# Tokens for the attention product: turned by VectorE in 32 by 32 blocks from a quartered load, instead of by TensorE

## The chip, the core and the metric

The kernel runs on one core of one Trainium2 chip. The metric is the device time of one launch in microseconds (us). Three runs of the kernel before gave 1968.97, 1972.87 and 1973.47 us; the median is 1972.87 us. All times below are from these runs or from one further execution that the hardware profiler recorded.

## What is computed

The reference takes x (4 batches of 1024 rows by 1024 features, float32) and a context (4 batches of 1024 by 512). Cut to what matters:

```python
query = ctx @ Wq.T + bq;  key = ctx @ Wk.T + bk            # 1024 x 128 for each batch
attention = softmax(query @ key.T, axis=-1)                # 1024 x 1024
x = x + einsum('bln,bmn->blm', layernorm(x), attention)    # rows l, features n and m
x = x + moe_ffn(layernorm(x))                              # shared and 8 routed experts
```

The rows of x are the tokens. Their features n are the index that the product with the attention sums over, so attention's second axis and the features of x must lie in the same order, whichever order that is. The normalisation is applied after the product: the raw x goes into the product, and the result is scaled by the row's reciprocal deviation and added to x minus its scaled mean.

## The kernel before, in words

The 4096 tokens are 32 tiles of 128 rows, numbered g. The first stage (some 640 us of the profile) makes attention and the product with it; the rest is the shared and the routed feed-forward network.

**The loop.** The first stage runs over pairs of token tiles, g = 0, 2, ..., 30; four pairs make a batch b. `product` (L399) multiplies the pair's two token tiles with the batch's attention by a scheme of seven block products instead of eight (`seven`, L197). Step k is eight matmuls of 128x512, into the PSUM banks pa, pc, pa, pb, pa, pc, pa. After step k VectorE adds the finished bank to x (L410, called "add k" below), and `between(k)` puts in the other work of the pair: the next batch's energies, softmax and turning of attention (`energies`, `softmax`, `turned`, only in the first three batches), the second normalisation and its turning of the previous pair (`second_norm` L426, `turn` L434), routing (`route` L460), lists, scatter. Since one bank serves several steps, step 4 needs add 2, step 6 needs add 4, and step 0 of the next pair needs add 6.

**Tokens.** TensorE sums over partitions, so a token tile must stand with features on partitions. `load(g)` (L374) reads the 128x1024 tile, rows on partitions. `tokens(g)` (L379) calls `transposed` (L250): eight TensorE transposes (L256) of 128x128 into two PSUM banks named pt_x, and two ScalarE copies (L260) of 128x512 into xT. `tokens(g + 1)` stands at the head of the pair (L611), `tokens(g + 2)` in `between(5)` (L684). `row_sums(g)` (L391, lines 176 to 179) then makes on GpSimd the four sums of the pair's blocks that the steps 1, 2, 4 and 5 use; it stands at the head of the pair (L613).

**After the add.** `stored(g)` (L421) follows add 5 and add 6: it writes the tile to x2d and takes its statistics on VectorE (L266 to 271); GpSimd makes rs and nb of them (L273, L275), and ScalarE the normalised tile xt (L430). `turn(g - 2)`, at the head of the next pair in the first three batches (L622), turns this xt on TensorE (pt_t). At the end of a batch VectorE also makes two sums of the next attention (L357, L362), and GpSimd two more (L367, L368).

**What sets the order.** On TensorE, GpSimd, VectorE and ScalarE each engine works in the order in which the code is written. The order of SP's queue, which issues all plain loads and stores, is set by a planner from its own costs; SP takes its entries one after the other and waits at each until what it needs is there. In the prologue (L540 to L587) SP loads weights, the first context blocks ct, constants, x, and gw_sb (L563), whose tile VectorE must have cleared first (L562).

The three lines that matter most:

```python
tokens(g + 1)              # L611, head of the pair
first_norm(g + 1)
a_units = row_sums(g)      # L613
```

Of the kernel before, what the change touches and what calls it, by code (L numbers as in the profile page):

```python
# [28 lines left out]
F32 = mybir.dt.float32  # L32
# [8 lines left out]
P = 128  # L41
B, S, D = 4, 1024, 1024
C = 512
T = B * S
NT = T // P
# [32 lines left out]
def xattn_moe_kernel(ctx: ExitStack, tc: tile.TileContext, x, ctxT, wqT, wkT, bqk, gwT, ebias,  # L78
                     w13, w2, w2t, sw13, sw2, sw2t, consts, out):
    nc = tc.nc  # L80
# [142 lines left out]


    HALF, KH, M = KC // 2, NF // 2, NF * P
    LT = S // P
    with ExitStack() as a:
        p1 = pool(attention, "p1")
# [7 lines left out]
        p4 = pool(two_sums, "p4", 1, "right")  # L236
# [13 lines left out]
        def transposed(dsts, src, n, second=None):  # L250

            for h, dst in enumerate(dsts):
                pt = ps_t.tile([P, HALF, P], F32, tag="pt", name=f"pt_{n}_{h}")
                for j in range(HALF):
                    c = h * HALF + j
                    nc.tensor.transpose(pt[:, j, :], src[:, c * P : (c + 1) * P], ident)  # L256
                if h and second:
                    nc.vector.tensor_copy(dst, pt)
                else:
                    nc.scalar.copy(dst, pt)  # L260
# [36 lines left out]
        def half_queries(b):  # L297
            for h in range(2):
                pq = ps_e.tile([P, 2, 2, 256], F32, tag="pe", name=f"pq_{b}_{h}")
                for j in range(2):  # L300
                    k = 2 * h + j
                    if (k, 0) not in contexts:
                        for i in range(2):
                            load_context(b, k, i)
                    ct = [contexts.pop((k, i)) for i in range(2)]
                    for i, w in enumerate((wq_sb, wk_sb)):
                        for c in range(CC):
                            nc.tensor.matmul(pq[:, i, j, :], w[c // CH][:, c % CH, :],  # L308
                                             ct[c // CH][:, c % CH, :],
                                             start=c == 0, stop=c == CC - 1)  # L310
                cols = slice(h * 512, (h + 1) * 512)
                for i, to in enumerate((qs, ks)):
                    nc.vector.tensor_scalar_add(
                        to[b][:, cols], pq[:, i].rearrange("p j n -> p (j n)"), bqk_sb[:, i : i + 1])
                yield

        def energies(b, m):
# [51 lines left out]
            t_sums[b] += four,  # L369


        xin, xTs, x1s, xts, norms = {}, {}, {}, {}, {}

        def load(g):  # L374
            x1 = p3.tile([P, D], F32, tag="x1", name=f"x1_{g}", bufs=4)
            nc.sync.dma_start(x1, x[g * P : (g + 1) * P, :])
            xin[g] = x1

        def tokens(g):  # L379
            xTs[g] = [p3.tile([P, HALF, P], F32, tag=f"x{g % 2}{h}", name=f"xT_{g}_{h}")  # L380
                      for h in range(2)]
            transposed(xTs[g], xin[g], f"x{g}")

        def first_norm(g):

# [164 lines left out]
            load_context(0, 1, i)  # L550
        nc.sync.dma_start(con, consts)
        load(0)
        with tc.manual_schedule(engines=vector_scalar):
            ps_e = psum("ps_e", 3)
            for dst, k in ((trib, "tri"), (onesb, "ones")):
                nc.vector.tensor_copy(dst, const(k))
            halves = queries(0)
            tokens(0)
            norms[0] = statistics(xin[0], "1_0")
            first_norm(0)  # L560
            gw_sb = wp.tile([P, KC, 32], F32, name="gw_sb")
# [7 lines left out]
            nc.sync.dma_start(eb_sb, ebias)  # L569
            next(halves)  # L570
            load(1)
            norms[1] = statistics(xin[1], "1_1")
            for m in range(LT + 2):
                if m < LT:
# [7 lines left out]
                if 0 < m <= LT:  # L582
                    scaled(0, m - 1, on_scalar=False)
            next(halves)
            first_sums(0)
            second_sum(0)
            ps_a.close()  # L587
# [3 lines left out]
            for p in range(NT // 2):  # L591
                g = 2 * p
                b, i = divmod(g, LT)
                ahead = b + 1 < B
                if g == NT - LT:

                    attention.close()
                    cps.append(pool(shared, "c0"))
                    sw13_sb = cps[0].tile([P, KC, W13], F32, name="sw13_sb")
                new = ahead and i == 0 and b > 0  # L600
                nms = {}

                def looked(m):
                    if ahead:
                        nms[m] = energies(b + 1, m)

                def softened(m):
                    if ahead:
                        softmax(b + 1, m, nms[m])

                tokens(g + 1)  # L611
                first_norm(g + 1)
                a_units = row_sums(g)  # L613
                if i == 0:
                    last_sums(b)
                if new:
                    halves = queries(b + 1)
                else:
                    looked(i)
                if p:  # L620
                    if ahead:
                        turn(g - 2)  # L622
                    second_norm(g - 1)
                if not new:
                    softened(i)

                def between(k):
                    if k == 0:
                        if not ahead:
                            turn(g - 2)  # L630
                        if new:
                            next(halves)
                        if p > 1:
                            pc_, ss, ohs = listing[g - 4]
                            listing[g - 4] = lists_of(g - 4, pc_, ohs), ss
                        if g + 2 < NT:
                            load(g + 2)
                            load(g + 3)
                        if g == NT - LT:
                            nc.sync.dma_start(sw13_sb, sw13)  # L640
                    elif k == 1:
                        if new:
                            looked(i)
                            softened(i)
                        if p:
                            turn(g - 1)
                        if ahead:
                            scaled(b + 1, i, on_scalar=True)
                        if p > 1:
                            tois, ss = listing.pop(g - 4)  # L650
                            listing[g - 4] = tois, [weighted(g - 4, j, ss) for j in range(G)]
                        if p in (1, 3, 5, 7, 10, 13):
                            convert((1, 3, 5, 7, 10, 13).index(p))
                    elif k == 2:
                        if not ahead:
                            pair[g] = gate_parts(g - 2)
                        looked(i + 1)
                        softened(i + 1)
                        if g + 2 < NT:
                            norms[g + 2] = statistics(xin[g + 2], f"1_{g + 2}")  # L660
                        if g + 2 == NT:
                            two_sums.close()
                            cps.append(pool(shared, "c3"))
                            block(0)
                    elif k == 3:
                        if p:
                            gs = gate_parts(g - 2) if ahead else pair.pop(g)
                            lg = ps_s.tile([P, G, E], F32, tag="lg", name=f"lg_{g}")
                        if ahead:
                            turned(b + 1, i)  # L670
                            scaled(b + 1, i + 1, on_scalar=True)
                        if p:
                            gate(lg, gs)
                            routing[g - 2] = route(g - 2, lg)
                        if p > 1:
                            scatter(g - 4, *listing.pop(g - 4))
                        if g + 2 < NT:
                            norms[g + 3] = statistics(xin[g + 3], f"1_{g + 3}")
                    elif k == 4:
                        if ahead:  # L680
                            turned(b + 1, i + 1)
                    elif k == 5:
                        if g + 2 < NT:
                            tokens(g + 2)  # L684
                        if p:
                            mask, ss, ohs = routing.pop(g - 2)
                            pc_ = ps_s.tile([P, 2, G, E], F32, tag="lg", name=f"pc_{g}")
                            counts(pc_, mask)
                            listing[g - 2] = pc_, ss, ohs
                        if ahead and i + 2 == LT:  # L690
                            first_sums(b + 1)
                        second_norm(g)
                        if g + 2 < NT:
                            first_norm(g + 2)
                    elif k == 6:
                        if ahead and i + 2 == LT:
                            second_sum(b + 1)

                product(g, b, a_units, between)


            last_in.close()
# [576 lines left out]
```

## Time and profile before

| what | value |
|---|---|
| median of three runs | 1972.87 us |
| the profiled execution | 1973.84 us |
| its span, first to last instruction | 1972.0 us |
| mean granted TensorE clock | 0.996 |
| busy: TensorE, VectorE, ScalarE, GpSimd | 98%, 41%, 26%, 33% |
| the first stage, 0 to 650 us: TensorE busy | 635.4 us |
| the first stage: VectorE, ScalarE, GpSimd busy | 384.7, 274.2, 251.3 us |
| DMA traffic | 365.48 MB |

The profile's page lists engines, the span in 40 slices, the chain of work that ended last, and groups of instructions with count, busy time and mean duration. A timeline lists instructions of one engine in order: start in us, duration in us, engine, source line, operation, output<-input, shape, count, and in square brackets how long the engine was idle just before and what released it. TensorE's matmuls are pipelined: the duration of one reaches past the start of the next, so the time that a group costs is the distance from its start to the next group's start.

### The profile page before, as it was taken

The numbers are of one execution on the slowest core, as the hardware profiler recorded it, in microseconds if no ns is written. First come the engines' busy times: TensorE is split into PE (matmuls) and PEld (weight loads), VectorE is DVE, ScalarE is ACT, GpSimd is POOL, SyncE is SP. The second block draws the span as 40 slices with busy tenths as digits, with TensorE's granted clock in tenths as the row PEclk, the third lists the DMA queues.
The fourth block names the chain that finished last, engine by engine and source line by source line (L and its number), as shares of the span: only waits on it lengthen the run. The fifth ranks groups of instructions, "written<-read, shape, count | busy, mean of one in ns | idle before, by whom it ended". The sixth has DMA issues, their size and how long they took to land.

```text
span 1972.0 us, 23197 instructions
## 1 busy us (share of the span) xinstructions
PE 1940.1 (98%) x8480; PEld 1155.5 (59%) x8595; DVE 810.4 (41%) x1981; ACT 512.9 (26%) x884; POOL 653.0 (33%) x598
## 2 busy tenths in 40 slices
PE   8999999999999999999999999999999999999997
PEld 5655655655444447676676758584845555446564
DVE  5556566565875325423132323222233333223343
ACT  3344354355334101010111101010102233223242
POOL 0423533543642140313231222313014454425454
PEclk9999999999999999999999999999999999999999
DMA  3276485437685225397777868596464598649995
GB/s 124 65 194 169 167 220 158 154 129 206 246 228 203 98 75 141 94 238 205 202 187 191 206 179 224 153 173 193 121 265 107 114 311 275 140 131 326 342 357 98
DMA packets 225040, 365.48 MB, mean 185 GB/s; under 512 B 114080, under 2 KB 169888, under 8 KB 214048
## 3 DMA queue, kind: packets, MB, share of 16 engines
q0 software_dynamic: 43024, 172.78, 32.8%
q1 hardware_dynamic: 181904, 191.21, 32.0%
q8 instruction: 69, 1.13, 0.2%
q14 instruction: 43, 0.35, 0.1%
HBM read 289.19 MB, written 174.59 MB: 235 GB/s over the span
## 4 chain that ended last, share of the span: by engine, by line
PE 89%; DMA 5%; SPq 2%; DVE 2%; issue 1%; ACT 0%; POOL 0%; POOLq 0%; DVEq 0%; ACTq 0%
PE pa L129 19%; PE bank L129 15%; PE pc L129 10%; PE bank L1151 8%; PE qa L129 6%; PE pb L129 5%; DMA xh<-xgt 4%; PE pu L129 4%; PE pq L308 3%; PE pe L320 3%; PE qc L129 3%; PE pt_c L129 2%; PE pt_a L256 2%; SPq L1004 2%; PE qb L129 1%; PE pt_t L256 1%
## 5 line engine op out<-in xcount | busy, mean ns | idle before, releaser
L129 PE MATMUL bank<-xTb,w 128*128 128x0 bf16 x2024 | 311.6, 315 | 2.1 <-ACT sg_b L145 1.3
L129 PEld LDWEIGHTS <-w 128*128 128x128 bf16 x2024 | 190.5, 98 | 111.5 <-DVE hTb L1135 1.3
L749 POOL DMA_INDIRECT xgt<-xrows,li x92 | 88.8, 965 | 444.2 <-DMA xh<-xgt 211.6
L1184 POOL DMA_INDIRECT out_dram<-yt,toks x92 | 147.7, 1605 | 139.5 <-DVE yt L1180 80.8
L1151 PE MATMUL bank<-w,hTb 128*128 128x0 bf16 x920 | 164.5, 326 | 0.1
L273 POOL TENSOR_TENSOR rs<-ve,con 128x1 f32<-128x1 f32 x64 | 47.8, 747 | 313.7 <-DVE ve L271 313.7
L146 DVE TENSOR_TENSOR hTb<-sg_b,bank 128x512 bf16<-128x512 f32 x115 | 78.8, 688 | 161.5 <-PE bank L129 157.2
L129 PE MATMUL pa<-xs,sw_sb 128*128 128x256 f32 x560 | 132.3, 379 | 0.0
L1151 PEld LDWEIGHTS <-hTb 128*128 128x128 bf16 x920 | 72.4, 98 | 87.4 <-issue 11.7
L129 PE MATMUL pa<-aT,xT 128*128 128x512 f32 x256 | 116.8, 599 | 2.2 <-DVE x L410 2.0
L129 PEld LDWEIGHTS pa<-xs,sw_sb 128*128 128x128 f32 x560 | 106.4, 190 | 14.5
L145 ACT ACTIVATE sg_b<-bank 128x512 f32<-128x512 f32 x115 | 68.5, 597 | 165.8 <-PE bank L129 150.2
L1180 DVE COPY yt<-bank 128x512 f32<-128x512 f32 x92 | 61.3, 689 | 121.9 <-PE bank L1151 112.5
L1182 ACT COPY yt<-bank 128x512 f32<-128x512 f32 x92 | 53.3, 587 | 144.1 <-PE bank L1151 131.7
L749 POOL DMA_INDIRECT w<-w13b,wi x23 | 23.0, 999 | 201.4 <-PE bank L129 153.6
L534 POOL DMA_INDIRECT xrows<-rr,toi x64 | 64.9, 1015 | 60.9 <-issue 45.3
L410 DVE SCALAR_TENSOR_TENSOR x<-pa,rs,x 128x512 f32<-128x512 f32 x64 | 47.9, 748 | 88.8 <-PE pa L129 82.9
L166 ACT ACTIVATE st_c<-pt_c 64x256 f32<-64x256 f32 x7 | 2.6, 378 | 311.0 <-PE pt_c L129 311.0
L266 DVE BATCH_NORM_STATS2 st<-x 128x6 f32<-128x512 f32 x128 | 81.8, 681 | 0.6
L1032 DVE TENSOR_TENSOR x2c<-x2c,qa 128x512 f32<-128x512 f32 x64 | 43.8, 685 | 92.4 <-PE qa L129 92.4
L129 PE MATMUL pu<-xb,sw_sb 128*128 128x512 f32 x176 | 76.3, 593 | 0.9 <-PE pt_t L256 0.9
L941 DVE TENSOR_TENSOR one<-one,pb 128x256 f32<-128x256 f32 x35 | 14.7, 421 | 149.4 <-PE pb L129 140.1
(262 smaller groups left out, 3346.5 us busy)
## 6 DMA issues: line engine op xcount, KB each, us to landing
xturned<-xh SPq DMA_DIRECT2D x46, 512.0 KB
xTb<-xturned SPq DMA_DIRECT2D x23, 1024.0 KB
w13b<-in_w_dram POOLq DMA_DIRECT2D x8, 2816.0 KB
x<-in_x_dram SPq DMA_DIRECT2D x32, 512.0 KB
x2d<-x SPq DMA_DIRECT2D x32, 512.0 KB
xtd<-xtT SPq DMA_DIRECT2D x16, 1024.0 KB
xb<-xtd SPq DMA_DIRECT2D x8, 2048.0 KB
x2c<-x2d SPq DMA_DIRECT2D x16, 1024.0 KB
```

Source lines behind the costliest of these rows:

```text
L129: nc.tensor.matmul(part(pp), w(c), part(xT(c)), start=start and c == 0, stop=c == blocks - 1, skip_group_check=not start)
L145: nc.scalar.activation(sg, pa, AF.Silu)
L146: nc.vector.tensor_tensor(hT[:, f, :], sg, pb, ALU.mult)
L256: nc.tensor.transpose(pt[:, j, :], src[:, c * P : (c + 1) * P], ident)
L266: nc.vector.bn_stats(st[:, h, :], src[:, h * 512 : (h + 1) * 512])
L308: nc.tensor.matmul(pq[:, i, j, :], w[c // CH][:, c % CH, :], ct[c // CH][:, c % CH, :], start=c == 0, stop=c == CC - 1)
L320: nc.tensor.matmul(pe[:, h, :], qs[b][:, m * P : (m + 1) * P], ks[b][:, h * 512 : (h + 1) * 512], start=True, stop=True)
L534: nc.gpsimd.indirect_dma_start(out=places[2 * (g + i) + k], out_offset=bass.IndirectOffsetOnAxis(ap=tois[k][:, i : i + 1], axis=0), in_=rr ...
L749: nc.gpsimd.indirect_dma_start(out=dst, out_offset=None, in_=src, in_offset=bass.IndirectOffsetOnAxis(ap=idx, axis=0), **bound)
L1151: nc.tensor.matmul(part(py), hT[:, f, toks], part(w[:, f, cols]), start=False, stop=f == NF - 1, skip_group_check=q < 2)
L1180: nc.vector.tensor_copy(yt[:, q, h * 512 : (h + 1) * 512], py)
L1184: adds.append([nc.gpsimd.indirect_dma_start(out=outs[q], out_offset=bass.IndirectOffsetOnAxis(ap=toks[:, q : q + 1], axis=0), in_=yt[:, q, ...
```

## The change

A second copy of each token tile is loaded, cut in four: partition 32j + a of the new tile xq holds, for i = 0 to 3, features 256j to 256j + 255 of row 32i + a. That takes four DMAs of 128 KB for each token tile. VectorE then turns each half of xq with one instruction of 128x512 that transposes every 32 by 32 block in place. The result stands in xT in another order of features: partition 32j + f of block c holds feature 256j + 32c + f. So that attention has the same order, the keys are written in that order when the bias is added to them. TensorE's transposes of x and ScalarE's copies are gone.

The places change too. Tokens for the next pair are now turned in `between(4)` and `between(5)`, the next pair's `row_sums` is called in `between(6)` instead of at its head, and the first two tiles are turned after the prologue instead of in it.

```diff
-                for i, to in enumerate((qs, ks)):
-                    nc.vector.tensor_scalar_add(
-                        to[b][:, cols], pq[:, i].rearrange("p j n -> p (j n)"), bqk_sb[:, i : i + 1])
+                nc.vector.tensor_scalar_add(
+                    qs[b][:, cols], pq[:, 0].rearrange("p j n -> p (j n)"), bqk_sb[:, :1])
+                nc.vector.tensor_scalar_add(
+                    ks[b].rearrange("p (c j f) -> p j c f", j=4, f=SQ)[:, 2 * h : 2 * (h + 1)],
+                    pq[:, 1].rearrange("p j (c f) -> p j c f", f=SQ), bqk_sb[:, 1:])
...
+        def load_quarters(g):
+
+            xqs[g] = xq = p4.tile([P, 4, D // 4], F32, tag="xq", name=f"xq_{g}", bufs=2)
+            src = x[g * P : (g + 1) * P, :].rearrange("(i a) (j f) -> j a i f", a=SQ, j=4)
+            for j in range(4):
+                nc.sync.dma_start(xq[j * SQ : (j + 1) * SQ], src[j])
+
         def tokens(g):
             xTs[g] = [p3.tile([P, HALF, P], F32, tag=f"x{g % 2}{h}", name=f"xT_{g}_{h}")
                       for h in range(2)]
-            transposed(xTs[g], xin[g], f"x{g}")
+            src = xqs.pop(g).rearrange("p i (h c f) -> p h i c f", h=2, f=SQ)
+            for h, dst in enumerate(xTs[g]):
+                nc.vector.transpose(dst.rearrange("p c (i a) -> p i c a", a=SQ), src[:, h])
...
         load(0)
+        load_quarters(0)
...
-            tokens(0)
...
             load(1)
+            load_quarters(1)
...
             next(halves)
+            tokens(0)
+            tokens(1)
+            units = [row_sums(0)]
             first_sums(0)
...
-                tokens(g + 1)
                 first_norm(g + 1)
-                a_units = row_sums(g)
...
                         if g + 2 < NT:
-                            load(g + 2)
-                            load(g + 3)
+                            for h in (g + 2, g + 3):
+                                load(h)
+                                load_quarters(h)
...
                     elif k == 4:
                         if ahead:
                             turned(b + 1, i + 1)
+                        if g + 2 < NT:
+                            tokens(g + 2)
                     elif k == 5:
                         if g + 2 < NT:
-                            tokens(g + 2)
+                            tokens(g + 3)
...
                     elif k == 6:
+                        if g + 2 < NT:
+                            units[0] = row_sums(g + 2)
...
-                product(g, b, a_units, between)
+                product(g, b, units[0], between)
```

More of the change, by code (lines that the diff above doesn't have):

```diff
@@ L225, in xattn_moe_kernel @@
     HALF, KH, M = KC // 2, NF // 2, NF * P
+    SQ = P // 4
     LT = S // P
@@ L369, in last_sums @@
             t_sums[b] += four,
-        xin, xTs, x1s, xts, norms = {}, {}, {}, {}, {}
+        xin, xqs, xTs, x1s, xts, norms = {}, {}, {}, {}, {}, {}
         def load(g):
```

## The prediction

> **What bounds the kernel now.** I read the engines' busy times, the chain that ended last, busy times by 50 us, and then the timelines of TensorE (PE), VectorE (DVE), ScalarE (ACT) and GpSimd (POOL) around the places that the change touches.
>
> ```profile
> PE 1940.1 (98%) x8480; PEld 1155.5 (59%) x8595; DVE 810.4 (41%) x1981; ACT 512.9 (26%) x884; POOL 653.0 (33%) x598
> ...
> PE 89%; DMA 5%; SPq 2%; DVE 2%; issue 1%; ACT 0%; POOL 0%; POOLq 0%; DVEq 0%; ACTq 0%
> ```
>
> TensorE is the chain. Between 100 and 500 us of the windows it is never idle, so work taken from it there is time won, as long as nothing else becomes late. The end of one pair (g = 4) and the start of the next, on TensorE:
>
> ```profile
> 159.54 1.04 PE L256 MATMUL pt_x<-con,x 128*128 128x128 f32 x8
> ...
> 160.47 3.68 PE L129 MATMUL pa<-t,xT 128*128 128x512 f32 x8
> 163.98 1.04 PE L256 MATMUL pt_x<-con,x 128*128 128x128 f32 x8
> 164.86 1.88 PE L320 MATMUL pe<-kT,qT 128*128 128x512 f32 x4
> 166.58 1.04 PE L256 MATMUL pt_t<-con,xt 128*128 128x128 f32 x8
> 167.45 3.60 PE L129 MATMUL pa<-aT,xT 128*128 128x512 f32 x8
> 170.88 3.60 PE L129 MATMUL pc<-t,s 128*128 128x512 f32 x8
> ```
>
> Eight transposes take 0.87 us (163.98 to 164.86), not eight times their 273 ns, since they are pipelined. What the other engines do then:
>
> ```profile
> 158.72 0.74 DVE L410 SCALAR_TENSOR_TENSOR x<-pa,rs,x 128x512 f32<-128x512 f32 x1
> 159.74 0.75 DVE L410 SCALAR_TENSOR_TENSOR x<-pc,rs,x 128x512 f32<-128x512 f32 x1 [0.28 <-PE pc L129]
> 160.41 1.28 DVE L266 BATCH_NORM_STATS2 st<-x 128x6 f32<-128x512 f32 x2
> ...
> 164.19 0.75 DVE L410 SCALAR_TENSOR_TENSOR x<-pa,rs,x 128x512 f32<-128x512 f32 x1 [1.94 <-PE pa L129]
> ```
>
> ```profile
> 167.61 1.27 POOL L176 TENSOR_TENSOR s<-xT,xT 128x512 f32<-128x512 f32 x1
> ```
>
> ```profile
> 163.12 1.24 ACT L430 ACTIVATE xt<-x,nb,rs 128x1024 f32<-128x1024 f32 x1 [1.87 <-POOL nb L275]
> ```
>
> VectorE is busy without a gap from routing (153.3) to add 4 (158.72); behind that it has 0.28 us to spare before add 5 and 1.94 before add 6. That is all the room for new work. The last batch, with no next attention to prepare, has less cover on TensorE. And the prologue:
>
> ```profile
> 15.70 1.04 PE L256 MATMUL pt_x<-con,x 128*128 128x128 f32 x8
> 16.58 1.89 PE L308 MATMUL pq<-ct,wq_sb 128*128 128x256 f32 x8
> ```
>
> ```profile
> 10.53 5.74 SPq L294 DMA_DIRECT2D ct<-in_ctxT_dram  x4
> 16.32 0.94 SPq L376 DMA_DIRECT2D x<-in_x_dram  x2
> 19.30 0.69 SPq L563 DMA_DIRECT2D gw_sb<-in_gwT_dram  x1
> ```
>
> Four context blocks are issued from 10.53 on, in time for TensorE at 16.58. The load of gw_sb comes later, at 19.30, when VectorE has cleared its tile (19.00 to 19.27).
>
> **The parts.** Listed in order, the built kernel has 256 transposes fewer on TensorE, 64 copies fewer on ScalarE, 64 transposes more on VectorE (two after add 4, two after the statistics that follow add 5), the same order on GpSimd, and 128 more DMAs on SP.
>
> *One VectorE transpose.* The trace has none. Bounds from rows of float32 on VectorE: below, half of a 1024-wide scaling from SBUF (L340, 754 ns), 0.38 us; above, one reduction of 1024 elements (L323, 1224 ns), 1.22 us, as if each element took two turns. Nearest is L266, which reads 512 elements from SBUF: 681 ns, two in a row 1.28 us. I take 0.70 us, and 1.3 us for the two of a tile.
> The trace has no transpose to weigh a rule against. The Trainium skill, "VectorE: DVE Perf Modes", The three transpose paths, gives VectorE 311 ns for 128x128 bf16 and TensorE 390 ns; its Rules for kernel authors send a 128x128 transpose to TensorE all the same. [...]
>
> *TensorE's saving.* 32 tiles x 0.87 = 27.8 us if all of it counted. Two tiles fall in the prologue, the rest at the 15 seams between pairs: 1.74 us each.
>
> *Eight usual seams (not at a batch's end, first three batches).* The first two transposes start at 159.4, so add 5 moves from 159.74 to 160.7, the statistics, nb and xt by the same 0.95: xt ends at 165.3 instead of 164.36. TensorE, 1.74 earlier, wants xt for pt_t at 164.84: it waits 0.5. Then add 6 follows the other two transposes, at 164.5 to 165.2, in time for step 0 at 166.2; GpSimd's first row sum ends 169.2, step 1 wants it at 169.65. Won: 1.74 - 0.5 = 1.2 us, eight times, **-9.6**.
>
> *The first seam (g = 0 to 2)* has no routing on VectorE: xt ends by 95.3, TensorE wants it at 95.9: **-1.7**. *The seams 6 to 8 and 14 to 16* have 6.9 us of context products on TensorE at their head as cover; but GpSimd's sums of attention start some 2 us later and hold up small VectorE work: L525 took 4.37 us instead of 0.75 beside L367 at 514.57. I charge 0.5 each: 2 x (1.74 - 0.5), **-2.5**.
>
> *Last batch.* At 22 to 24 step 0 waits for add 6, which follows two transposes and L357: 503.21 becomes 505.4. Nothing covers it: **+2.2**, and the row sums behind it shift alike. At 24 to 26 VectorE is behind: add 4 ends 533.3 and the transposes go straight onto add 5, the statistics and add 6, while TensorE idles: +1.15. At 26 to 28 and 28 to 30 add 6 ends 0.2 later than the old transposes let step 0 start. Together **+3.75**.
>
> *Prologue.* In the new order of SP the load of gw_sb stands ahead of the four context blocks. It still waits for VectorE's clear at 19.27, which itself follows the first key and the statistics of tile 0. So the blocks are issued from about 20.5, not 10.53. The first load of the trace took 2.5 us from the end of its issue (1.62) to its first matmul (4.15); I add the same: TensorE goes on at 23.4 instead of 16.58, **+6.8** (bounds: 5.7 if the block lands in 1.4 us, 8.5 if the 1024 small packets of gw_sb hold it up). TensorE is then idle for 7.7 us. The only idle time so long is the start, and after it eight matmuls took 3.62 us at 8.58 and 1.89 us at 13.98; if it comes back so, 2 to 4 us are lost, if not, none: I take **+2**.
> The Trainium skill, "TensorE: Matmul & The Clock Gate", Why this matters for your kernels, says that a gap of over 3 us between bursts halves the clock again; the rows of the start agree with a slow beginning, and no row here shows it after a gap; by that rule and the start's 8 us the loss is 4.
> After the loop, four transposes (2.6 us) stand before L357, which step 1 needs: GpSimd and VectorE then share out L357, L362 and the row sums as at 64 to 71 us, and steps 1 and 2 come 0.55 late each, **+1.1**. The two old transposes of the prologue win nothing: the first lies in the new gap, the second in a wait for kT (0.72 us at 64.58).
>
> *Without cost:* the 128 DMAs (16.8 MB). SP issues one in 0.33 us, 8 a pair 2.7 us, in a queue that issues five in 34.5 us. The tile loads are issued by some 171 us and used after 181 (statistics) and 193 us (transposes); if the weight conversions that fill the DMA engines at 180 to 190 us took this cover of 10 us, the price would be VectorE standing still, and TensorE with it. ScalarE loses 34 us that nobody waits for. The key's new order is the same 0.74 us.
>
> Sum: -9.6 - 1.7 - 2.5 + 3.75 + 6.8 + 2 + 1.1 = -0.15 us. The profiled execution took 1973.84 us, 1.0 above the median of the three runs; against the median this is **1973 us**: no change, though the stage is another.
>
> **Rivals.** (1) *Slower: float32 costs VectorE two turns an element,* 1.22 us a transpose. For it: 32 by 32 blocks must be filled before they are read out. Against it: nothing on VectorE here with 512 elements takes over 0.75. Each 0.1 us above 0.70 costs 0.2 at eight seams, 0.4 at four and 0.4 in the prologue, 3.6 us; at 0.52 more, with the first row sum late too (8 x 0.5), +23: 1996 us. It is slower by over 0.3% (5.9 us, about what a measurement of this kernel can tell from no change) from 0.86 us a transpose. (2) *Faster: the prologue is covered.* If the context blocks land sooner and the clock stays, 3 us less; with transposes at 0.55, 5 us less; with the seams of the last batch hidden, up to 3 less: 1964 us. (3) *A load becomes the wait:* gw_sb's packets hold the first blocks (+1.7), the clock takes its full 4 us (+2), and the extra traffic costs each of 15 pairs 0.4 us of VectorE (+6): 1983 us. That transposes stay on TensorE is excluded by the listed order.
>
> **How the numbers follow.** Forecast (within 5.9 us) 0.45, rival 1 0.17, rival 2 0.20, rival 3 0.18. The forecast's own range is 1967 to 1979. The range for 8 in 10 takes in the faster case from 1963 and the slower ones up to 1992, leaving out the worst of rival 1. Faster by over 0.3% 0.20, within 0.3% 0.43, slower 0.37 (rivals 1 and 3 and a little of the forecast's edge).
>
> **What would show it.** Right: a gap of 6 to 9 us on TensorE near 16 to 24 us, released by a DMA of ct; pair periods of some 33.3 us instead of 34.5 in the first three batches, with a wait of about 0.5 us of pt_t for xt; waits for add 6 of 2 us and more at the start of pairs 24 and 26; VectorE transposes near 0.70 us. Wrong: transposes over 0.86 us, waits of VectorE for xq or x, or no gap in the prologue.

## The result, and the profile after

The changed kernel takes 1972.01 us (median of 20 runs, 1968.35 to 1976.57); 20 runs of the kernel before, on the same chip, have a median of 1971.86 us. The ratio is 1.0002, with a 95% interval of 0.9995 to 1.001: no difference. The profiled execution took 1972.87 us, its span is 1971.1 us against 1972.0, and the stage that the change touches ended 1.1 us earlier (the first shared product starts at 626.94 instead of 628.02). TensorE has 256 instructions and 23 us of work less, and nearly all of it came back as waiting.

The page of the changed kernel, engines and the chain that ended last:

```profile
PE 1916.8 (97%) x8224; PEld 1126.5 (57%) x8339; DVE 860.0 (44%) x2045; ACT 480.6 (24%) x820; POOL 645.6 (33%) x598
...
PE 82%; DVE 8%; DMA 4%; ACT 2%; issue 2%; SPq 1%; POOL 1%; POOLq 0%; DVEq 0%
```

TensorE had 89% of the chain and VectorE 2%; now they have 82% and 8%. A seam between two pairs (g = 4 to 6), TensorE and then VectorE of the changed kernel (start, duration, engine, line, operation; in brackets the idle time and what ended it):

```profile
165.52 3.70 PE L132 MATMUL pa<-t,xT 128*128 128x512 f32 x8
169.06 1.88 PE L326 MATMUL pe<-kT,qT 128*128 128x512 f32 x4
171.23 1.09 PE L260 MATMUL pt_t<-con,xt 128*128 128x128 f32 x8 [0.29 <-ACT xt L445]
172.16 3.60 PE L132 MATMUL pa<-aT,xT 128*128 128x512 f32 x8
```

```profile
164.72 0.74 DVE L425 SCALAR_TENSOR_TENSOR x<-pa,rs,x 128x512 f32<-128x512 f32 x1
165.38 1.29 DVE L397 STREAM_TRANSPOSE xT<-xq 128x512 f32<-128x512 f32 x2
166.60 0.71 DVE L425 SCALAR_TENSOR_TENSOR x<-pc,rs,x 128x512 f32<-128x512 f32 x1
167.23 1.27 DVE L270 BATCH_NORM_STATS2 st<-x 128x6 f32<-128x512 f32 x2
...
169.09 1.30 DVE L397 STREAM_TRANSPOSE xT<-xq 128x512 f32<-128x512 f32 x2
170.32 0.71 DVE L425 SCALAR_TENSOR_TENSOR x<-pa,rs,x 128x512 f32<-128x512 f32 x1
```

Both pt_x groups are gone from TensorE; in their place it waits 0.29 us for xt, which is late because add 5 (166.60) stands behind the first two transposes. The seam still wins: from one step 0 to the next, pairs 4 to 6, 34.66 us became 33.36. The prologue, SP's queue and then TensorE:

```profile
6.22 2.55 SPq L390 DMA_DIRECT2D xq<-in_x_dram  x4
17.77 0.68 SPq L578 DMA_DIRECT2D gw_sb<-in_gwT_dram  x1
18.50 0.65 SPq L584 DMA_DIRECT2D eb_sb<-in_ebias_dram  x1
19.24 1.93 SPq L298 DMA_DIRECT2D ct<-in_ctxT_dram  x4
```

```profile
12.45 1.89 PE L312 MATMUL pq<-ct,wk_sb 128*128 128x256 f32 x8
22.07 3.70 PE L312 MATMUL pq<-ct,wq_sb 128*128 128x256 f32 x8 [7.73 <-DMA ct<-in_ctxT_dram]
25.60 1.89 PE L312 MATMUL pq<-ct,wk_sb 128*128 128x256 f32 x8
```

The four context blocks are issued at 19.24 instead of 10.53, behind gw_sb. TensorE stands still for 7.73 us and goes on 5.5 us later than in the kernel before (16.58), and the eight matmuls after it take 3.70 us where their neighbours take 1.89. And the last batch, the starts of products that wait:

```profile
499.67 5.40 PE L132 MATMUL pa<-aT,xT 128*128 128x512 f32 x8 [4.37 <-DVE x L425]
520.69 5.26 PE L132 MATMUL pa<-aT,xT 128*128 128x512 f32 x8 [2.03 <-DVE x L425]
...
594.29 5.40 PE L132 MATMUL pa<-aT,xT 128*128 128x512 f32 x8 [1.86 <-DVE x L425]
```

Eight matmuls of 512 columns take 3.70 us elsewhere. That a slower clock is meant, and not late data, is seen in the busy times by stretch (columns: stretch, its length, then busy time and count of each engine; the column PEclk is the one number without a count after POOL's):

```profile
22.07:25.60 3.53, 3.53 (x8) 2.85 (x9) 0.00 (x0) 0.00 (x0) 0.00 (x0) 0.51 0.93 294
25.60:27.33 1.73, 1.73 (x10) 1.52 (x8) 0.00 (x0) 0.00 (x0) 0.00 (x0) 1.00 1.04 224
...
499.70:505.10 5.40, 5.40 (x10) 2.33 (x11) 3.86 (x6) 0.69 (x1) 3.50 (x3) 0.68 0.97 400
594.30:599.70 5.40, 5.40 (x10) 2.33 (x11) 1.68 (x5) 3.40 (x4) 3.32 (x5) 0.68 0.24 97
```

The granted clock is 0.51 after the gap of 7.73 us, 0.68 over the eight matmuls after the waits of 4.37 and 1.86 us, and 1.00 otherwise.

The start of step 0 of each pair, after minus before, read from the two timelines of TensorE, is the account of the whole stage:

| stretch | difference added | forecast |
|---|---|---|
| prologue, up to pair 0 | +8.06 | +8.8 |
| pair 0 to 2 (one seam; steps 1 and 2 late) | -0.69 | -1.7 + 1.1 |
| eight usual seams | -10.67 | -9.6 |
| 6 to 8 and 14 to 16 | -3.51 | -2.5 |
| last batch, pair 22 to the end | +5.73 | +3.75 |
| sum | -1.08 | -0.15 |

### The profile page after: what moved, and what is told of

Its sections match the earlier page's. It is cut to its first block, busy times and chain, and to the rows that moved or that the text cites. A ratio compares the mean times of both kernels' runs of the same rounds, so it can differ in the third digit from the quotient of the medians.

```text
span 1971.1 us, 22853 instructions
## 1 busy us (share of the span) xinstructions
PE 1916.8 (97%) x8224; PEld 1126.5 (57%) x8339; DVE 860.0 (44%) x2045; ACT 480.6 (24%) x820; POOL 645.6 (33%) x598
## 4 chain that ended last, share of the span: by engine, by line
PE 82%; DVE 8%; DMA 4%; ACT 2%; issue 2%; SPq 1%; POOL 1%; POOLq 0%; DVEq 0%
PE pa L132 17%; PE bank L132 15%; PE pc L132 8%; PE bank L1173 8%; PE qa L132 6%; PE pb L132 5%; PE pu L132 4%; PE pq L312 3%; PE qc L132 3%; PE pt_c L132 2%; DMA xh<-xgt 2%; PE pe L326 2%; DVE st L270 2%; PE qb L132 1%; PE pt_t L260 1%
## 5 line engine op out<-in xcount | busy, mean ns | idle before, releaser
L277 POOL TENSOR_TENSOR rs<-ve,con 128x1 f32<-128x1 f32 x64 | 41.7, 652 | 314.5 <-DVE ve L275 311.1
L132 PE MATMUL pa<-aT,xT 128*128 128x512 f32 x256 | 121.8, 620 | 11.6 <-DVE x L425 11.6
L132 PEld LDWEIGHTS pa<-aT,xT 128*128 128x128 f32 x256 | 48.0, 198 | 64.4 <-issue 51.2
```

What stands on the lines that cost most here:

```text
L132: nc.tensor.matmul(part(pp), w(c), part(xT(c)), start=start and c == 0, stop=c == blocks - 1, skip_group_check=not start)
```

## The experiments

The theory: the seams win some 15 us, and the prologue (gw_sb ahead of the context blocks) and the last batch (VectorE's chain with no cover on TensorE) give it back, each by a wait and by a slow TensorE behind it. The rivals: the 128 loads cost; VectorE had room and the loss is elsewhere; the seams win nothing. Eleven kernels ran; ratios are to the kernel before, run on the same chip with them.

**1. gw_sb late.**

```diff
-            gw_sb = wp.tile(...); nc.vector.memset(gw_sb, 0.0); nc.sync.dma_start(gw_sb[:, :, :E], gwT)
...
             next(halves)
             load(1)
             load_quarters(1)
             norms[1] = statistics(xin[1], "1_1")
+            gw_sb = wp.tile(...); nc.vector.memset(gw_sb, 0.0); nc.sync.dma_start(gw_sb[:, :, :E], gwT)
```

> The changed kernel, with the clearing of gw_sb and its load written behind the second half of the queries and the statistics of tile 1, so that the four context blocks stand ahead of gw_sb in SP's queue. Theory (the 8 us at the first pair come from gw_sb holding up the context blocks, and from TensorE's slow start after that gap): the gap of 7.7 us and the 3.70 us of the first eight matmuls after it are gone, step 0 of pair 0 comes at 66 to 67.5 us instead of 74.4, and all of it stays to the end: 1962 to 1965 us, 0.9950 to 0.9965 of the kernel before. Rival A (the context blocks are late for another reason, such as the four quarter loads ahead of them): step 0 of pair 0 stays above 71 us and the time above 1968. Rival B (the time won early is waited away later): step 0 of pair 0 early, time near 1972.

Measured: 1965.11 us, ratio 0.9966 (0.9952 to 0.9979). SP's queue and TensorE of this kernel:

```profile
8.48 0.45 SPq L580 DMA_DIRECT2D eb_sb<-in_ebias_dram  x1
9.79 4.68 SPq L298 DMA_DIRECT2D ct<-in_ctxT_dram  x4
```

```profile
16.05 3.68 PE L312 MATMUL pq<-ct,wq_sb 128*128 128x256 f32 x8 [1.97 <-DMA ct<-in_ctxT_dram]
```

Step 0 of pair 0 comes at 68.41 instead of 74.43 (I had expected 66 to 67.5), and of the 6.02 us won 5.80 are still there at pair 30. That settles the first half: the place of one load of gw_sb in SP's queue cost 6 us. The other 2.0 us at pair 0 have two sources, seen in the timelines. The first is the slow clock: the matmuls at 16.05 start 0.5 us earlier than those at 16.58 of the kernel before, but cost 1.8 us more. The second is the key's new order. The kernel before, and then this one, at the first energies (`pe`, queries times keys):

```profile
23.49 1.02 PE L320 MATMUL pe<-kT,qT 128*128 128x512 f32 x2
25.15 4.56 PE L320 MATMUL pe<-kT,qT 128*128 128x512 f32 x10 [0.65 <-DVE kT L313]
```

```profile
26.41 5.42 PE L326 MATMUL pe<-kT,qT 128*128 128x512 f32 x12 [1.50 <-DVE kT L318]
```

Each half of the keys is now spread over all 1024 columns, so no energies can start on the first half alone. From the last keys' matmuls to the first `pt_a` it is 9.27 us instead of 8.52: 0.75 us. The kernel of experiment 2 has the late blocks with the old order of keys, and has its two early matmuls and the 8.52 us. Three later kernels with the prologue of experiment 1 start pair 0 at 68.74, 68.92 and 66.84. The third has no slow matmuls behind its wait (2.85 us), and only 0.5 us are left; the first has slow instructions at 47.92, the second at 16.57. So 0.75 us are the key's order, and some 1.7 us of slow clock vary from run to run.

**2 and 3. The loads alone,** added to the kernel before with nothing reading them, first with gw_sb where it was written, then with gw_sb late.

```diff
+            xq = p4.tile([P, 4, D // 4], F32, tag="xq", name=f"xq_{g}", bufs=2)
+            for j in range(4):
+                nc.sync.dma_start(xq[j * SQ : (j + 1) * SQ], src[j])
```

> The kernel before with the 128 quarter loads added and nothing reading them; the transposes stay on TensorE. In its listed order on SP the load of gw_sb stands ahead of the context blocks, as in the changed kernel. Theory: the prologue alone is harmed, by about 8 us at step 0 of pair 0 (74 instead of 66.4), the pairs keep their 34.6 us: 1979 to 1982 us, 1.0035 to 1.005. Rival (the 128 loads themselves cost, by traffic or SP's queue, some 0.4 us a pair): 1985 us or more. Rival (the gap comes with VectorE's transposes): 1972.

> The kernel before with the 128 quarter loads added and nothing reading them, and with gw_sb cleared and loaded late, so that the context blocks go first. Theory: the loads cost nothing and the prologue is whole: 1971 to 1974 us, ratio 0.999 to 1.001, step 0 of pair 0 at 66 to 68 us. Rival (traffic costs 0.4 us a pair): 1978 us.

Measured: 1984.54 us, ratio 1.0073 (1.0059 to 1.0087), and 1980.25 us, ratio 1.0044 (1.0031 to 1.0057). Both are slower than my theory, the second by over 6 us. The step 0 starts tell why: the usual seams keep their 34.58 us, so no price by traffic of 0.4 us a pair; but from pair 8 to 10 they take 47.18 and 46.57 instead of 43.20 us, since context blocks come late. The second kernel there:

```profile
214.11 1.10 PE L309 MATMUL pq<-ct,wq_sb 128*128 128x256 f32 x4 [2.54 <-DMA ct<-in_ctxT_dram]
```

```profile
209.00 0.35 SPq L377 DMA_DIRECT2D x<-in_x_dram  x1
209.44 0.89 SPq L295 DMA_DIRECT2D ct<-in_ctxT_dram  x2
210.38 0.46 SPq L385 DMA_DIRECT2D xq<-in_x_dram  x1
```

Again it is the order of SP's queue, which the planner made anew: quarter loads stand between stores and context blocks. The first block is issued at 209.44, 2.1 us before TensorE wants it. In the changed kernel it is issued 8.4 us before (205.19), and this seam (8 to 10) shows no such wait and takes 41.87 us. The stage explains 5.3 of the second kernel's 8.5 us in the profiles; the rest lies after the stage and stays open. (From the first shared product to the end the profiles of all these kernels take 1342.2 to 1347.2 us, with the same code; differences of a few us in the total are no evidence about the stage.) Between these two kernels gw_sb's place makes 4.3 us by the medians and 5.5 us at pair 0.

**4. The last batch's transposes all behind add 2.**

```diff
                         if g + 2 < NT:
                             norms[g + 2] = statistics(xin[g + 2], f"1_{g + 2}")
+                            if g >= 22:
+                                tokens(g + 2)
+                                tokens(g + 3)
...
-                        if g + 2 < NT:
+                        if g + 2 < NT and g < 22:
                             tokens(g + 2)
...
-                        if g + 2 < NT:
+                        if g + 2 < NT and g < 22:
                             tokens(g + 3)
```

> The changed kernel, with the transposes of the four last seams (22 to 24 and on) put behind add 2, ahead of the first statistics of the next tiles, instead of behind add 4 and add 5. Theory (5.7 us are lost between pair 22 and the end of the attention products because add 5, the statistics and add 6 queue behind these transposes, with TensorE waiting and starting slowly): the waits of step 0 for add 6 fall from 4.4, 1.6, 1.8, 1.9 us to at most 2.2, 0.5, 0.7, 0.7, and the time is 1966 to 1968.5 us, 0.997 to 0.9985. Rival (the last batch waits for GpSimd's sums and for transfers, whatever VectorE's order): within 1 us of 1972.

Measured: 1979.17 us, ratio 1.0038 (1.0024 to 1.0053): wrong, in sign too. The first of the four seams did what I expected (22 to 24: 32.30 us instead of 34.77). (The kernel has the transposes behind the first statistics that follow add 2, not ahead of them as the expectation says.) In pairs 24 and 28 the wait moved (39.07 and 34.08 us from step 0 to step 0 instead of 34.92 and 30.12). TensorE and VectorE of this kernel in pair 24:

```profile
528.91 6.38 PE L132 MATMUL pa<-t,xT 128*128 128x512 f32 x8 [3.28 <-DVE x L425]
```

```profile
519.62 2.49 DVE L397 STREAM_TRANSPOSE xT<-xq 128x512 f32<-128x512 f32 x4
522.03 0.71 DVE L425 SCALAR_TENSOR_TENSOR x<-pb,rs,x 128x512 f32<-128x512 f32 x1
```

Four transposes ahead of add 3 make routing and add 4 late, and step 6 waits for add 4: 3.28 us, and 2.7 more for the slow matmuls (6.38 instead of 3.68). I had looked at the end of VectorE's chain and not at its middle.

**5. One tile's transposes moved into an idle place** (with gw_sb late): at 22 to 24 both tiles as in the last experiment, at the other three seams the first tile behind add 2's statistics, the second where it was. In pairs 26 and 28 VectorE of the kernel before had 2.12 us of idle time there, ahead of add 3; in pair 24 it had none.

```diff
+                            if g >= NT - LT - 2:
+                                tokens(g + 2)
+                            if g == NT - LT - 2:
+                                tokens(g + 3)
...
-                        if g + 2 < NT:
+                        if g + 2 < NT and g < NT - LT - 2:
                             tokens(g + 2)
...
-                        if g + 2 < NT:
+                        if g + 2 < NT and g != NT - LT - 2:
                             tokens(g + 3)
```

> The kernel with gw_sb late (1965 us), and in the last batch the transposes where VectorE had idle time before: at the seam 22 to 24 both tiles behind the statistics that follow add 2; at the later three seams the first tile there and the second behind the statistics that follow add 5, where it is now. Theory (what the change loses in the last batch is VectorE's chain between routing and add 6; with one tile moved into the 2 us of idle time ahead of add 3, add 6 waits no more than before): seam 22 to 24 2.5 us shorter, the others 0.5 to 1 us each: 1959 to 1962 us, 0.993 to 0.995. Rival (GpSimd's sums or the scatters set the pace there): the waits of step 0 move to another releaser and the time stays at 1964 to 1966. The earlier version, with all four transposes of a pair behind add 2, lost more at add 4 than it won at add 6.

Measured: 1963.91 us, ratio 0.9956 (0.9942 to 0.997): above the 1959 to 1962 that I expected. From step 0 of pair 22 to the first shared product: 156.31 us in the kernel before, 162.04 after the change, 162.14 with gw_sb late alone, 157.47 here. So 4.6 of the 5.7 us are gone. Most of it is the seam 22 to 24 (2.5 us) and pair 30, whose first matmuls run at full speed (3.70 us) again; the seam 26 to 28 gives 0.8, and 24 to 26 loses 0.3 (35.17 us). The 1.7 us of pair 30 aren't surely VectorE's order: experiment 8 has the changed kernel's order there, the same wait of 1.86 us, and full speed behind it. The other 2.9 us are. The waits of all steps for adds, from 480 to 640 us, of the changed kernel and of this one (us in total, times, longest):

```profile
PE pa L132 <- DVE x L425: 11.9, 6, 4.4
```

```profile
PE pa L132 <- DVE x L425: 8.6, 7, 2.0
```

The kernel before has 2.0 us there, and had TensorE's transposes as cover. By the total times alone the gain can't be told from none: this ratio and that of gw_sb late alone differ by 0.001, with intervals of 0.0014 each way.

**6. Each transpose twice,** on the changed kernel.

> The changed kernel with each VectorE transpose made twice in a row, the second over the first: VectorE works 1.3 us more for a tile, 2.6 for a pair. Theory (the transposes stand in the chain add 4, add 5, statistics, add 6 with almost nothing to spare, so each further 0.1 us costs what the forecast priced, 3.6 us): 24 us more than the changed kernel, and up to 32 if the whole 2.6 us count in the last batch: 1994 to 2004 us, ratio 1.011 to 1.016; waits of pt_t for xt of 1 us and more and of step 0 for add 6 at usual seams. Rival (VectorE has room there, and the change gave its gain back in other places only): below 1980 us.

Measured: 2020.67 us, ratio 1.0242 (1.0222 to 1.0262), twice the price that I gave. A usual seam of this kernel:

```profile
338.37 1.10 PE L260 MATMUL pt_t<-con,xt 128*128 128x128 f32 x8 [1.66 <-ACT xt L446]
339.71 3.70 PE L132 MATMUL pa<-aT,xT 128*128 128x512 f32 x8 [0.25 <-DVE x L426]
343.66 3.70 PE L132 MATMUL pc<-t,s 128*128 128x512 f32 x8 [0.24 <-POOL s L179]
```

Pairs 12 to 14 take 35.73 us instead of 33.23: of 3.0 us more work on VectorE 2.5 count, in three waits. (VectorE's busy time rose from 860.0 to 907.4 us, 3.0 us a pair.) In the last batch the seams from pair 22 to 30 take 16.5 us more in all, where VectorE does 11.9 more; three waits of 4.5 to 6.9 us and one of 1.82 us also slow the matmuls behind them (5.37 to 6.63 us instead of 3.70). So VectorE has next to no room, and the rival that it does is out.

**7. No turning at all** (with gw_sb late): the rows are loaded straight into xT.

```diff
-            for j in range(4):
-                nc.sync.dma_start(xq[j * SQ : (j + 1) * SQ], src[j])
+            for h, dst in enumerate(xTs[g]):
+                nc.sync.dma_start(dst.rearrange("p c t -> p (c t)"),
+                                  x[g * P : (g + 1) * P, h * 512 : (h + 1) * 512])
```

> The kernel with gw_sb late, with no transpose of the tokens at all: the rows of x are loaded straight into the tiles that should hold their transposes, so the product is made of untransposed tokens and the turning is left out. It prices VectorE's 64 transposes as a whole. Theory: a usual seam then saves what TensorE gave up, 1.74 us of 34.58 (periods of 32.8 to 32.9 instead of 33.2), the seams of the last batch have no VectorE transposes ahead of add 6, and the first pair loses 0.3 us or less behind step 0: the attention products end 9 to 11 us earlier than with gw_sb late alone (621.2), at 610 to 612 us. Rival (VectorE's transposes cost little beside other limits): periods of 33.2 as now, end at 617 or later. The time after the products depends on where the tokens are routed and isn't compared.

Measured: 1966.31 us, ratio 0.9967 (0.9954 to 0.9979); the products end at 621.48. The seam is as expected, and so are the first steps (pair 0 to 2 takes 30.10 us, with no wait):

```profile
311.00 1.88 PE L326 MATMUL pe<-kT,qT 128*128 128x512 f32 x4
312.72 1.04 PE L260 MATMUL pt_t<-con,xt 128*128 128x128 f32 x8
313.59 3.60 PE L132 MATMUL pa<-aT,xT 128*128 128x512 f32 x8
```

No wait, and 32.83 us from pair 12 to 14: all 1.75 us that TensorE gave up. The end isn't as expected: the new order of SP's queue makes context blocks late at the pairs 8 and 16 (waits of 6.3 us in two), and 8 to 10 and 16 to 18 take 46.21 and 46.56 us where the changed kernel takes 41.87 and 41.92. That is 9 us more together, about as much as I had looked for, so the end doesn't show the gain. At pair 8 an x load that waits 4.9 us for a store stands ahead of the blocks, and the first block is issued 4.9 us before TensorE wants it, not 8.4.

**8 and 9. Both tiles behind add 5's statistics** in the first three batches, with gw_sb late, and then with the last batch placed as in experiment 5.

```diff
                     elif k == 4:
...
-                        if g + 2 < NT:
-                            tokens(g + 2)
                     elif k == 5:
                         if g + 2 < NT:
+                            tokens(g + 2)
                             tokens(g + 3)
```

> The kernel with gw_sb late, with both tiles' transposes of the first three batches behind the statistics that follow add 5, none between add 4 and add 5; the last batch as in the changed kernel. Theory (TensorE's wait of 0.2 to 0.3 us for xt at each usual seam is there because add 5 and so xt stand behind the first transposes; moved behind, xt is early and add 6 comes no later): 0.2 to 0.3 us less at each of some 11 seams, 1961 to 1963.5 us, 2 to 3 us under the 1965 of the kernel with gw_sb late alone. Rival (add 6 or the first row sum becomes the wait as soon as xt is none): within 1 us of 1965 or above.

> All three together: gw_sb late, both tiles' transposes behind add 5's statistics in the first three batches, and the last batch's transposes in VectorE's idle time. Theory: the gains add up, 1956 to 1960 us, 0.992 to 0.9945 of the kernel before. Rival (the stages share one limit, GpSimd's sums): not under 1962.

Measured: 1967.41 us, ratio 0.9976 (0.9966 to 0.9986), and 1965.69 us, ratio 0.9972 (0.996 to 0.9983). Both are above what I expected. The wait for xt is gone, and nothing is won: pairs 12 to 14 take 33.19 us, and with the last batch placed the products end at 616.16 instead of 616.74, although pair 0 starts 1.9 us earlier. GpSimd of the first of the two shows where it went:

```profile
314.51 0.55 POOL L277 TENSOR_TENSOR rs<-ve,con 128x1 f32<-128x1 f32 x1 [4.22 <-DVE ve L275]
315.13 0.19 POOL L279 TENSOR_TENSOR nb<-ve,rs 128x1 f32<-128x1 f32 x1
315.27 1.26 POOL L179 TENSOR_TENSOR s<-xT,xT 128x512 f32<-128x512 f32 x1
```

The first row sum stands behind rs and nb of the tile of add 6 and ends at 316.53; step 1 wants it at 316.34.

**10 and 11. The first two tiles in idle time of the prologue** (with gw_sb late and experiment 5), and then all of it, with the row sums ahead of that rs in GpSimd's queue.

```diff
+            tokens(0)
             eb_sb = wp.tile([P, E], F32, name="eb_sb")
...
+            tokens(1)
             next(halves)
-            tokens(0)
-            tokens(1)
             units = [row_sums(0)]
```

> The kernel with gw_sb late and the last batch's transposes in VectorE's idle time, and the first two tiles' transposes in its idle time of the prologue too (tile 0 behind the statistics of tile 0, tile 1 ahead of the second half of the next queries), instead of behind those queries. Theory (steps 1 and 2 of the first product come 0.2 to 0.6 us late each since four transposes stand ahead of the first difference of attention): pair 0 to pair 2 takes 30.1 us instead of 31.1, the products end 1 us earlier than 616.7, time 1961 to 1964. Rival (the first row sums and the difference contend for the same port whatever the order): pair 0 to pair 2 stays at 31.1.

> The same, and in the first three batches both tiles' transposes behind add 5's statistics, with the row sums of the next pair issued ahead of the square root of the tile stored after add 6 in GpSimd's queue. Theory (in the version with both behind add 5 the wait for xt went, but the row sums stood behind rs and nb of that tile and step 1 waited 0.2 us for the first of them): neither wait is left, seam periods of 32.85 to 33.0 us instead of 33.2, the products end at 612 to 614 us, time 1958 to 1962. Rival (the row sums ahead make nb and so the second xt late, and pt_t waits behind step 1): periods of 33.2 or more, 1963 or more.

Measured: 1962.38 us, ratio 0.9943 (0.993 to 0.9957), and 1963.25 us, ratio 0.995 (0.9936 to 0.9964). In the first, pair 0 to 2 takes 30.09 us (expected 30.1), but the products end at 616.31, 0.4 us earlier than in experiment 5 and not 1. In the second the usual seam takes 32.83 us from 12 to 14, exactly that of the kernel with no turning, and has no wait. Its GpSimd now starts on the row sums as soon as VectorE is done:

```profile
308.82 1.27 POOL L179 TENSOR_TENSOR s<-xT,xT 128x512 f32<-128x512 f32 x1 [1.82 <-DVE xT L397]
```

But SP's queue is in another order again, context blocks come late at two pairs (3.5 us of waits), and the products end at 615.62 instead of 612 to 614. The eleventh stays above its range. The tenth has the lowest median, 0.57% under the kernel before, interval 0.43% to 0.70%; those of several others, the fifth and the eleventh among them, overlap it.

## Why the prediction was right

The time was right, and so were the two sides of the sum and where each came from. That the sum came out within 1 us is in part luck: the seams gave 2.2 us more than forecast and the prologue took 0.7 us less, the last batch took 2.0 us more, and some of that varies from run to run.

*One transpose at 0.70 us, two at 1.3:* 671 ns and 1.29 to 1.30 us. Nearest row right. The Trainium skill, "VectorE: DVE Perf Modes", Rules for kernel authors, sends a 128x128 transpose to TensorE; here TensorE's eight took 0.87 us and VectorE's two, for the same data, 1.3. The trace agrees with the rule in that TensorE takes less time for it; the seam was still shorter with the work on VectorE, because TensorE was the chain.

*Usual seams, -1.2 each:* -1.33 on average; the wait for xt is 0.17 to 0.29, not 0.5. Experiment 7, without the turning, shows the whole 1.75. *Seams 6 to 8 and 14 to 16, -2.5:* -3.51; the 0.5 each that I charged for GpSimd's sums beside small VectorE work did not come. *First seam and late steps:* right (-0.69 together, forecast -0.6), and experiment 10 shows that the lateness was the order that I named.

*Last batch, +3.75:* +5.73. The waits were right in place, and the first two seams lost 2.5 and 1.0 us (forecast 2.2 and 1.15). The second is in part luck: it has two slow restarts (1.7 and 1.6 us) that I hadn't charged, and lacks a wait of 1.4 us for the row sums that the kernel before has; the wait for add 6 at pair 26 was 1.64 us, not 2 and more. What I left out is that TensorE comes back slow from some waits: another 1.7 us in pair 30, behind a wait of 1.86 us. One more thing was not foreseen: in pair 28 VectorE waited twice, 2.2 and 2.3 us, for the scatter's buffer.

*Prologue, +6.8 and +2:* 8.06 in all: 5.5 for the gap (TensorE went on at 22.07, not 23.4), 1.8 for the slow matmuls, and 0.75 for the key's order. That last term I had put at nothing: the forecast has only the duration of VectorE's instruction (0.74 us as before), not which energies can start behind it. Experiment 1 gives 6.0 to gw_sb, so the mechanism is shown.

*The 128 loads at nothing:* right in the changed kernel, where VectorE never waits for xq. But in experiments 2, 3, 7 and 11 the context blocks came late: a re-made order of SP's queue can put an entry that waits ahead of them. I had named traffic as the risk, and the queue's order only for gw_sb.

*Rival 1's price, 3.6 us for 0.1 us of a transpose:* mis-sized by a factor of nearly two. In experiment 6 each transpose cost VectorE 0.74 us more, and 47 us for 0.74 us is 6.4. I had counted one tile of the two at a usual seam, 1.6 us in all for eight; they cost 3.3, so most of both counts. The forecast hung on the 0.70 us more than I said: by 6.4 us, an estimate, slower by 0.3% begins near 0.76 us, not at 0.86.

## What to carry to other kernels

Work taken from the engine that bounds a kernel is won only where what takes its place has cover; list the places by stage, and look at the prologue and at the last round, which have none. In an order that a planner makes, adding loads moves other loads: read the new queue entry by entry for one that waits for an engine, with needed loads behind it. Put moved work where its engine was idle, and check who waits in the middle of the chain, not only at its end.

## What the runs showed of the hardware

TensorE's slow restart comes after shorter waits than I had thought, and not each time. In these eleven kernels, the kernel before and the changed one, up to 640 us, no wait of 1.0 to 1.76 us had slow instructions behind it. Of the waits from 1.82 to 2.04 us 12 of 20 did. The same wait of 1.86 us at pair 30 was followed by 5.40 us for eight matmuls in the changed kernel and by 3.70 in experiment 8; the same wait of 2.03 us in pair 24 by 5.26 in the changed kernel and by 3.67 in the kernel before. Three of 2.54 to 2.85 us (experiments 3, 9 and 11) had none; every other from 2.87 us on did. One wait of 1.78 or 1.79 us in the prologue is in all thirteen profiles, with slow instructions behind it in two; three more of 1.78 to 1.80 us elsewhere had none. Here it is in experiment 9, without them, and in experiment 5, with them:

```profile
47.70 1.06 PE L260 MATMUL pt_a<-con,at 128*128 128x128 f32 x8 [1.78 <-DVE at L346]
```

```profile
47.92 1.66 PE L260 MATMUL pt_a<-con,at 128*128 128x128 f32 x8 [1.78 <-DVE at L346]
```

The granted clock of the second is 0.59 (47.92 to 49.60). Behind a slow restart eight matmuls of 128x512 took 1.4 to 2.9 us more. The Trainium skill, "TensorE: Matmul & The Clock Gate", HAM oscillation — how this bites in real kernels, has gaps above some 3.4 us as what brings the slow clock back; these runs show it from 1.78 us on in some executions. Why one execution has it and another not stays open.

VectorE's float32 transpose of 128x512 in blocks of 32 by 32 takes about as long as another pass over 512 elements: 671 ns (median), against 678 ns for one statistics instruction.
